# Layer 0's last hidden chunk: a split moved forward, the last sums by output chunk, one written order for three engines

## The chip, the cores and the metric

The kernel runs on one core of a Trainium2 chip, in one launch. The metric is the device time of that launch in microseconds (us): 423.62 us before, the median of three runs (423.48 to 424.63). The engines are called PE (matmul), PEld (its weight loads), DVE (vector), ACT (scalar), POOL and SP. POOL and SP do little here but issue DMAs.

## The reference, cut to what matters

Eight sequences of 128 tokens with 512 features, so 1024 rows, go through two layers:

```python
# layer 0: a linear map with low-rank experts, then a gated FFN with 4-bit weights
c = x @ W.T + low_rank(x)                        # 512 features
g, u = split(c @ dequant(qweight_gu))            # 1376 hidden units each
x = x + (silu(g) * u) @ dequant(qweight_down)
# layer 1: one of 8 matrices for each sequence, RMS norm, then a gated FFN
a = x[b] @ weight[adapter_ids[b]].T
x = x + (silu(n(a) @ gate_w.T) * (n(a) @ up_w.T)) @ down_w.T     # 1792 hidden units
```

## The kernel before

All activations lie feature by row: `xT` is 128 partitions x 4 feature chunks (`KC = 4`) x 1024 rows. The rows are two blocks (`NTB = 2`) of 512 (`TB`). Products are made in rounded halves: a value is split in a high part (ACT) and a low part (DVE), and each product is then two matmuls, one for each part.

The hidden units of layer 0 are 11 chunks of 128 (the last one has 96). For a chunk j, `gu_products` sums gate and up over four feature chunks c, four matmuls for one of gate or up at one c (two parts by two row blocks). The scales of the 4-bit weights differ from one c to the next, so between two c the sum in PSUM is multiplied in place (`rescale`) by a ratio, on ACT or DVE, whichever has the smaller load by the planner's own costs. After the last c, `gu_final` makes the silu on ACT (L675) and the product with up on DVE (L678): this is h(j). `queue_split` puts the two halves of h(j)'s split into the queues of ACT (high part, L323) and DVE (low part, L313). A queued step is written where `pump` finds room for it, or where `flush(name)` demands it at the latest.

The down sums of chunk k are added to four PSUM tiles (one for each output chunk m, with two banks, one for each row block). `down_product` makes four matmuls for one m and one k: both parts by both row blocks. `rescale` stands between two k here too. `down_final` (L719) adds the finished sum to `xT` on DVE.

The function `last_chunk_and_down` interleaves the last chunk's gate and up (j = 10) with the last block of down sums (k = 8, 9, 10). There are four pairs of PSUM banks in all, and gate, up, and the sums of m = 0 and 1 take them; m = 2 gets gate's pair when silu has read it, m = 3 gets up's pair when h(10) is made. Its order is: c = 0; `first(0)` (the products of k = 8 for m = 0 and their rescale); c = 1; `first(1)`; c = 2; `second(0)` (k = 9); c = 3; `second` and `first` for the rest; the split of h(10); a table load on ACT (L776); and at last the products of k = 10, by row block and then by m, each with a final of 512 columns.

Layer 1 begins with eight `adapt` products (L1261, float32), one for each sequence, into single PSUM banks that are the halves of the old pairs. A row's sum goes through a square sum (ACT L1277), a root, a reciprocal (DVE L1286), a scaling (ACT "nx" L1199), four transposes (PE L1302), and a norm. The order of all this, and of the chunk work behind it, comes from a planner (`Plan.run`) that knows a cost and a due time for each task; the first weight splits of layer 1 (L1069 on ACT, L1072 and L1075 on DVE) are ready to run early and fill DVE around the seam of the layers. `sums_of_weights` (L1065, L1066) adds rows of a raw weight buffer on DVE; it needs an accumulating DMA (`add_to_raw`, L1062) that POOL issues. There are three raw buffers, raw0 to raw2. POOL issues the loads of layer 1's matrices too (`load_w1`, L397), into four buffers w1_0 to w1_3; w1_3's place is that of layer 0's h and comes free with the last down product.

What sets the order of the instructions: within a `tc.manual_schedule` the order on PE, DVE and ACT is that of the code, or that in which the planner calls the tasks. SP's and POOL's orders are a scheduler's. There are two such contexts, one for all of layer 0 and one for `plan.run()`.

Of the kernel before, what the change touches and what calls it, by code (L numbers as in the profile page):

```python
# [14 lines left out]
F32 = mybir.dt.float32  # L15
# [8 lines left out]
P = 128  # L24
B, T, D = 8, 128, 512
NT = B * T
TB = 512
# [186 lines left out]
def network_in(ctx, tc, a, out, by_groups, flag, again):  # L214
# [23 lines left out]

    cond_stack, h_stack, w1_stack, ad_stack = (ExitStack() for _ in range(4))
    cp = cond_stack.enter_context(tc.tile_pool(name="cond", bufs=1, side="right"))  # L240

    def behind(inst, other):

# [44 lines left out]
    def spent(n):  # L288

        base = clock[0]  # L290
        clock[0] += 0.2326 * n
        pump(base, clock[0] + OVER)

    def rescale(ps, by):
        n = ps.free_size()
        engine = min(load, key=lambda e: max(load[e], clock[0] + AFTER) + took(e, n))
        charge(engine, took(engine, n))
        if engine == "act":
            nc.scalar.activation(ps, ps, AF.Copy, scale=by)  # L299
        else:  # L300
            nc.vector.tensor_scalar(ps, ps, by, None, ALU.mult)
# [271 lines left out]
    def by_groups_of_scales():  # L573
# [126 lines left out]
                        if half == 1:  # L700
                            queue_split(f"h{j}", h, h2[j])

        def down_product(ps, m, k, first, tbs=range(NTB)):
            n = CH0[k]
            for i in range(2):
                for tb in tbs:
                    nc.tensor.matmul(  # L707
                        ps[:, tb],
                        lhsT=wds[k][:n, m * P : (m + 1) * P],
                        rhs=h2[k][i][:, tb],  # L710
                        start=(first and i == 0),
                        stop=(i == 1),
                        skip_group_check=not first,
                    )
            spent(2 * len(tbs))

        def down_final(x, m, ps, group):
            charge("dve", took("dve", ps.free_size()))
# [16 lines left out]
        def last_chunk_and_down():  # L735
# [35 lines left out]
            for m in range(2, KC):  # L771
# [7 lines left out]
            second(1, range(1, NTB))  # L779
            for m in range(2, KC):  # L780
                second(m)
            for tb in range(NTB):
                for m in range(KC):
                    down_product(sums[m], m, j, False, range(tb, tb + 1))
                    down_final(xT[:, m, tb * TB : (tb + 1) * TB], m, sums[m][:, tb], group)

        def split_condition(tb, ps, i):

# [25 lines left out]
            return count  # L814


        with tc.manual_schedule(engines={EngineType.PE, EngineType.DVE, EngineType.Activation}):

            nc.scalar.activation(root, eps, AF.Exp)
            exp0 = experts(0)  # L820
            x_high(0)
            x_low(0)
            x_scaled(0)
            exp1 = experts(1)
            for m in range(2):
                w_high(m)
            hg0 = gated(0, rows_of(exp0))
            for m in range(2, KC):
                w_high(m)
            kept = cp.tile([P, 2, 2 * (E + E * R)], F32, name="kept")  # L830
            nc.scalar.copy(kept, exp1[:, :, : 2 * (E + E * R)])
            x_high(1)
            scale_bT()
            pairs0, base0 = base_sums()
            for m in range(KC):
                base_products(base0, 0, m, 0)
            hgT0 = turned(hg0, exp0[:, 0, :])
            for m in range(KC):
                w_low(m)
                base_products(base0, 0, m, 1)  # L840
            x_low(1)
            x_scaled(1)
            for ps in pairs0:
                rescale_base(ps)
            pairs1, base1 = base_sums()
            for i in range(2):
                for m in range(KC):
                    base_products(base1, 1, m, i)
            x_diff(0)
            for m in range(KC):  # L850
                w_diff(m)
                base_products(base0, 0, m, 2)
            hg1 = gated(1, [kept[:, i].rearrange("p (b n) -> p b n", b=2) for i in range(2)])
            for ps in pairs1:
                rescale_base(ps)
            x_diff(1)
            queue_zeros(0, 4, "zeros")
            for j in range(4):
                queue_weights(j, f"w{j}")
            flush("w0")  # L860
            for i in range(2):
                for m in range(2 * i, 2 * i + 2):
                    low_rank(base0, hgT0, m)
                split_condition(0, pairs0[i], i)
            ratios(ratio, sc)
            flush("w1")
            ratios(ratio_d, scd)
            for m in range(2):
                base_products(base1, 1, m, 2)
            hgT1 = turned(hg1, base0[0])  # L870
            base_products(base1, 1, 2, 2)
            for i in range(2):
                for m in range(2 * i, 2 * i + 2):
                    if m == KC - 2:
                        base_products(base1, 1, KC - 1, 2)
                    low_rank(base1, hgT1, m)
                split_condition(1, pairs1[i], i)
                if i == 0:
                    for _ in range(2):
                        run("dve", 0)  # L880
            cond_stack.close()
            open_rw()
            pools["w1"] = w1_stack.enter_context(tc.tile_pool(name="w1", bufs=1, side="right"))
            hp = h_stack.enter_context(tc.tile_pool(name="h0", bufs=1, side="right"))
            load_down(*BLOCKS0[0])
            for pair0 in PAIRS0[2:4]:
                load_qw(*pair0)

            def dequantise(pair0, zeros=None):
                if zeros is not None:  # L890
                    queue_zeros(*zeros, "zeros")
                for j in range(*pair0):
                    queue_weights(j, f"w{j}")

            def ready(pair0):
                for j in range(*pair0):
                    flush(f"w{j}")

            load["act"], load["dve"] = clock[0] + 1.0, clock[0] + 2.0

            queue_down(*BLOCKS0[0], "d0", at=clock[0] + 7.0)
            gate_up_pair(0, 1)
            ready(PAIRS0[1])
            dequantise(PAIRS0[2], (4, 8))
            gate_up_pair(2, 3)
            flush("d0")
            load_down(*BLOCKS0[1])
            dequantise(PAIRS0[3])
            queue_down(*BLOCKS0[1], "d4", at=clock[0] + 6.0)
            down(*BLOCKS0[0])  # L910
            ready(PAIRS0[2])
            load_qw(*PAIRS0[4])
            gate_up_pair(4, 5)
            ready(PAIRS0[3])
            load_qw(*PAIRS0[5])
            flush("d4")
            load_down(*BLOCKS0[2])
            dequantise(PAIRS0[4], (8, 10))
            first_raw()
            gate_up_pair(6, 7)  # L920
            dequantise(PAIRS0[5], (10, 11))
            queue_down(*BLOCKS0[2], "d8")
            queue("dve", "indices", 1.7, indices)
            down(*BLOCKS0[1])
            flush("indices")
            first_w1()
            ready(PAIRS0[4])
            gate_up_pair(8, 9)
            ready(PAIRS0[5])
            count = []  # L930
            queue("dve", "verdict", 1.3, lambda: count.append(verdict()))
            queue_first_weights("l1")
            last_chunk_and_down()
            flush("verdict")
            flush("l1")

            def met(ps):
                nc.tensor.matmul(ps[:1, :1], lhsT=count[0][:, 0:1], rhs=count[0][:, 1:2], start=True, stop=True)

            def told(ps):  # L940
                nc.vector.tensor_scalar(flag[:1], ps[:1, :1], float(NGOOD * P), None, ALU.is_lt)

            judges.append((met, told))


    def in_float32():
# [852 lines left out]
```

## Time and profile before

| | |
|---|---|
| median of three runs | 423.62 us (423.48 to 424.63) |
| the profiled execution's own time | 423.74 us |
| its span in the trace | 421.9 us, granted PE clock 0.995 |
| PE busy | 411.8 us (98%) |
| DVE busy | 373.0 us (88%) |
| ACT busy | 307.0 us (73%) |
| layer 0's last chunk and down sums | about 144.8 to 165.6 us of the span |
| layer 1's eight rows (adapt, norm, transposes) | about 165.6 to 205 us |
| layer 1's chunks | about 205 us to the end |

1.84 us of the profiled time lie outside the span. Stretches and single instructions are told in us from the span's start. A line of the timeline gives start, duration, engine, line, operation, output and inputs, shape and count; the bracket at its end is the idle time of that engine ahead of it, and what ended the idle time. A PE line's end is modelled, and short stalls of PE show better on PEld, whose next load can't start while it waits for a semaphore.

### The profile page before, as it was taken

The numbers are of one execution on the slowest core, as the hardware profiler recorded it, in microseconds if no ns is written. First come the engines' busy times: TensorE is split into PE (matmuls) and PEld (weight loads), VectorE is DVE, ScalarE is ACT, GpSimd is POOL, SyncE is SP. The second block draws the span as 40 slices with busy tenths as digits, with TensorE's granted clock in tenths as the row PEclk, the third lists the DMA queues.
The fourth block names the chain that finished last, engine by engine and source line by source line (L and its number), as shares of the span: only waits on it lengthen the run. The fifth ranks groups of instructions, "written<-read, shape, count | busy, mean of one in ns | idle before, by whom it ended". The sixth has DMA issues, their size and how long they took to land.

```text
span 421.9 us, 5201 instructions
## 1 busy us (share of the span) xinstructions
PE 411.8 (98%) x1771; PEld 314.9 (75%) x1771; DVE 373.0 (88%) x678; ACT 307.0 (73%) x503; POOL 27.1 (6%) x34
## 2 busy tenths in 40 slices
PE   8999999999999999999999999999999999999993
PEld 8885778888888765445676777788778877887772
DVE  4799979997998689989999999988998899979963
ACT  5833798868796765668998787658975797669651
POOL 1000200000000300320011011011011001000000
PEclk9999999999999999999999999999999999999997
DMA  8931811010010720870163035033323134000014
GB/s 271 394 144 36 233 56 44 11 53 2 0 62 2 278 46 18 329 239 2 58 181 62 0 87 138 0 87 88 113 50 89 62 75 114 0 3 1 24 51 155
DMA packets 16913, 38.59 MB, mean 91 GB/s; under 512 B 1904, under 2 KB 8432, under 8 KB 15856
## 3 DMA queue, kind: packets, MB, share of 16 engines
q1 hardware_dynamic: 11344, 25.09, 17.8%
q0 software_dynamic: 4960, 12.06, 11.5%
q10 hardware_dynamic: 576, 1.05, 0.6%
q8 instruction: 15, 0.25, 0.2%
q14 instruction: 18, 0.15, 0.1%
HBM read 36.10 MB, written 2.10 MB: 91 GB/s over the span
## 4 chain that ended last, share of the span: by engine, by line
PE 85%; DVE 8%; ACT 4%; issue 1%; ACTq 0%; DVEq 0%
PE bank L1446 27%; PE bank L1585 17%; PE gate L659 9%; PE up L659 9%; PE down L707 8%; PE base L510 5%; PE bank L1261 5%; PE experts L413 2%; PE base L536 2%; DVE w L1072 1%; DVE xT L719 1%; DVE w L1075 1%; PE idle L366 1%; PE bank L1302 1%; DVE snap L1534 1%
## 5 line engine op out<-in xcount | busy, mean ns | idle before, releaser
L1199 ACT ACTIVATE bank<-bank 128x512 f32<-128x512 f32 x129 | 73.3, 584 | 31.9 <-PE bank L1446 17.6
L1585 PE MATMUL bank<-h,d 128*128 128x512 f32 x240 | 66.5, 391 | 0.2
L1585 PEld LDWEIGHTS bank<-h,d 128*128 128x128 f32 x240 | 44.8, 188 | 10.6 <-DVE snap L1480 0.6
L659 PE MATMUL gate<-a,dq 128*128 128x512 f32 (+1 forms) x176 | 47.8, 393 | 0.1
L659 PE MATMUL up<-a,dq 128*128 128x512 f32 (+1 forms) x176 | 47.4, 391 | 0.0
L1446 PE MATMUL bank<-xs,w 128*128 128x512 f32 x168 | 46.0, 396 | 0.8 <-ACT bank L1199 0.8
L1446 PE MATMUL bank<-a,w 128*128 128x512 f32 x168 | 45.2, 394 | 0.2 <-ACT snap L1199 0.2
L707 PE MATMUL down<-h,wd 128*128 128x512 f32 (+1 forms) x176 | 42.6, 395 | 0.6 <-DVE h L313 0.4
L707 PEld LDWEIGHTS down<-h,wd 128*128 128x128 f32 (+1 forms) x176 | 32.4, 188 | 10.0 <-DVE xT L719 1.3
L659 PEld LDWEIGHTS gate<-a,dq 128*128 128x128 f32 (+1 forms) x176 | 32.5, 185 | 8.5 <-ACT sl L675 0.6
L659 PEld LDWEIGHTS up<-a,dq 128*128 128x128 f32 (+1 forms) x176 | 32.4, 185 | 7.9 <-DVE a L791 0.4
L1446 PEld LDWEIGHTS bank<-xs,w 128*128 128x128 f32 x168 | 31.1, 188 | 9.1 <-ACT bank L1199 1.6
L1446 PEld LDWEIGHTS bank<-a,w 128*128 128x128 f32 x168 | 30.7, 188 | 9.0 <-ACT snap L1199 2.2
L1075 DVE SCALAR_TENSOR_TENSOR w<-w 128x512 fp32r<-128x512 f32 x50 | 34.5, 690 | 2.1
L299 ACT ACTIVATE gate<-gate,ratio 128x1024 f32<-128x1024 f32 (+1 forms) x24 | 26.1, 1086 | 10.7 <-PE gate L659 10.7
L1480 DVE SCALAR_TENSOR_TENSOR snap<-bank,snap 128x512 f32<-128x512 f32 x42 | 28.6, 684 | 4.9 <-ACT wz L1069 4.8
L1072 DVE TENSOR_TENSOR w<-raw,w 128x512 fp32r<-128x512 f32 x42 | 28.7, 684 | 3.1 <-ACT w L1069 3.1
L1062 POOL DMA_DIRECT2D raw<-in_wgu x14 | 17.4, 1246 | 208.2 <-PE gate L659 45.6
L1624 DVE SCALAR_TENSOR_TENSOR xT<-bank,xT 128x512 f32<-128x512 f32 (+1 forms) x41 | 27.4, 672 | 3.0 <-PE bank L1585 2.6
L1585 PE MATMUL bank<-w,d 128*128 128x512 f32 x96 | 29.4, 391 | 0.0
L1261 PE MATMUL bank<-w,xT 128*128 128x512 f32 x64 | 29.2, 596 | 0.0
L1199 ACT ACTIVATE snap<-bank 128x512 f32<-128x512 f32 x41 | 24.2, 593 | 5.9 <-PE bank L1446 5.8
(169 smaller groups left out, 736.9 us busy)
## 6 DMA issues: line engine op xcount, KB each, us to landing
raw<-in_wgu SPq DMA_DIRECT2D x14, 640.0 KB, 4.0
raw<-in_wgu POOLq DMA_DIRECT2D x14, 256.0 KB, 4.4
wd<-in_wd SPq DMA_DIRECT2D x14, 256.0 KB, 2.7
qw<-in_qw_gu SPq DMA_DIRECT2D x5, 512.0 KB, 4.7
xT<-in_xT SPq DMA_DIRECT2D x2, 1024.0 KB, 12.2
out<-xT SPq DMA_DIRECT2D x7, 256.0 KB, 2.0
xb<-in_xb ACTq DMA_DIRECT2D x4, 256.0 KB, 5.2
xb<-in_xb SPq DMA_DIRECT2D x4, 256.0 KB, 5.2
```

The costliest lines, as they stand in the source:

```text
L299: nc.scalar.activation(ps, ps, AF.Copy, scale=by)
L510: nc.tensor.matmul(base[m], lhsT=wT3[i][:, m, c * P : (c + 1) * P], rhs=x_parts(tb)[i][:, c, :], start=(i == 0 and c == 0), stop=(i == 1 a ...
L659: nc.tensor.matmul(ps, lhsT=dqs[j][:, c, half, :], rhs=a3[i][:, c, tb * TB : (tb + 1) * TB], start=(c == 0 and i == 0), stop=(i == 1), ski ...
L707: nc.tensor.matmul(ps[:, tb], lhsT=wds[k][:n, m * P : (m + 1) * P], rhs=h2[k][i][:, tb], start=(first and i == 0), stop=(i == 1), skip_gro ...
L1072: nc.vector.tensor_tensor(lo, raw, hi.bitcast(F32), ALU.subtract)
L1075: nc.vector.scalar_tensor_tensor(di, lo.bitcast(F32), -1.0 / EPS, hi.bitcast(F32), ALU.mult, ALU.add)
L1199: nc.scalar.activation(out_, in_, AF.Copy, scale=by)
L1261: nc.tensor.matmul(of("bank", "ad", b), lhsT=xT[:, c, b * T : (b + 1) * T], rhs=of("w1", b)[:, c * D : (c + 1) * D], start=(c == 0), stop= ...
L1446: nc.tensor.matmul(ps, lhsT=w[:, i, n, c * P : (c + 1) * P], rhs=x[i][:, c0 + c], start=(first and i == which[0] and c == 0), stop=True, s ...
L1480: nc.vector.scalar_tensor_tensor(x, of("bank", j, bank_), by, x, ALU.mult, ALU.add)
L1585: nc.tensor.matmul(of("bank", *who), lhsT=of("d", j)[:, i, m * P : (m + 1) * P], rhs=h_tile(j, tb)[:, i], start=(i == 0 and j == j0), stop ...
L1624: nc.vector.scalar_tensor_tensor(x, of("bank", *who)[:, q * w : (q + 1) * w], -EPS, x, ALU.mult, ALU.add)
```

## The change

Three edits. (1) In `last_chunk_and_down`, the products of `first(0)` are parted: those with h(8)'s high part stay behind c = 0, those with its low part go behind c = 1. The split of h(9) is demanded ahead of c = 1, where it was demanded ahead of `second(0)`. And `second(0)` is parted by row blocks: one half stands ahead of the last gate products, the other ahead of the last up products. (2) The last products (k = 10) go by m and not by row block first: four matmuls for an m, then its final over 1024 columns at once; only m = 3 has two finals of 512. (3) One `manual_schedule` is opened at layer 0's start and closed behind `plan.run()`; the code between keeps its order.

```diff
+    order_stack = ExitStack()
+
+    def written_order():
+        engines = {EngineType.PE, EngineType.DVE, EngineType.Activation}
+        order_stack.enter_context(tc.manual_schedule(engines=engines))
...
-        def down_product(ps, m, k, first, tbs=range(NTB)):
+        def down_product(ps, m, k, first, tbs=range(NTB), parts=range(2)):
...
-            def gate_up(c):
-                for half, ps in enumerate(gu):
+            def gate_up(c, halves=range(2)):
+                for half in halves:
+                    ps = gu[half]
...
-            def first(m):
-                down_product(sums[m], m, j - 2, True)
-                rescale(sums[m], ratio_d[:, m, j - 2 : j - 1])
+            def first(m, parts=range(2)):
+                down_product(sums[m], m, j - 2, True, parts=parts)
+                if 1 in parts:
+                    rescale(sums[m], ratio_d[:, m, j - 2 : j - 1])
...
             gate_up(0)
-            first(0)
+            first(0, range(1))
+            flush(f"h{j - 1}")
             gate_up(1)
+            first(0, range(1, 2))
             first(1)
             gate_up(2)
             flush(f"h{j - 1}")
-            second(0)
-            gate_up(3)
+            second(0, range(1))
+            gate_up(KC - 1, range(1))
+            second(0, range(1, NTB))
+            gate_up(KC - 1, range(1, 2))
...
-            for tb in range(NTB):
-                for m in range(KC):
-                    down_product(sums[m], m, j, False, range(tb, tb + 1))
-                    down_final(xT[:, m, tb * TB : (tb + 1) * TB], m, sums[m][:, tb], group)
+            for m in range(KC):
+                down_product(sums[m], m, j, False)
+                if m < KC - 1:
+                    down_final(xT[:, m, :].rearrange("p (b t) -> p b t", b=2), m, sums[m], group)
+                else:
+                    for tb in range(NTB):
+                        down_final(xT[:, m, tb * TB : (tb + 1) * TB], m, sums[m][:, tb], group)
...
-        with tc.manual_schedule(engines={EngineType.PE, EngineType.DVE, EngineType.Activation}):
+        written_order()
...
-    with tc.manual_schedule(engines={EngineType.PE, EngineType.DVE, EngineType.Activation}):
-        plan.run()
+    if not by_groups:
+        written_order()
+    plan.run()
+    order_stack.close()
```

How that moves instructions, by the order of the two programs, engine by engine. PE: the parted products, and the last sixteen by m. DVE: the low part of h(9) stands right behind that of h(8), ahead of the rescale of gate's second sum (c = 1) and of the down rescale of m = 0, which change places too; and the "di" step of a layer 1 weight split (L1075) that stood behind the eight finals stands ahead of the five. ACT: one high part of a layer 1 weight split (L1069) goes two instructions later. POOL: the accumulating DMA into raw2, which was issued ahead of w1_3's first load, is issued behind it. SP is the same, and so is everything in layer 1 on PE, DVE and ACT.

More of the change, by code (lines that the diff above doesn't have):

```diff
@@ L701, in gate_up_pair @@
                             queue_split(f"h{j}", h, h2[j])
-        def down_product(ps, m, k, first, tbs=range(NTB)):
+        def down_product(ps, m, k, first, tbs=range(NTB), parts=range(2)):
             n = CH0[k]
-            for i in range(2):
+            for i in parts:
                 for tb in tbs:
@@ L714, in down_product @@
                     )
-            spent(2 * len(tbs))
+            spent(len(parts) * len(tbs))
         def down_final(x, m, ps, group):
@@ L814, in verdict @@
             return count
-        with tc.manual_schedule(engines={EngineType.PE, EngineType.DVE, EngineType.Activation}):
[L819 to L834, printed above, removed]
-            for m in range(KC):
[L836 to L858, printed above, removed]
-                queue_weights(j, f"w{j}")
[L860 to L943, printed above, removed]
@@ new lines, in by_groups_of_scales @@
+        written_order()
+        nc.scalar.activation(root, eps, AF.Exp)
+        exp0 = experts(0)
+        x_high(0)
+        x_low(0)
+        x_scaled(0)
+        exp1 = experts(1)
+        for m in range(2):
+            w_high(m)
+        hg0 = gated(0, rows_of(exp0))
+        for m in range(2, KC):
+            w_high(m)
+        kept = cp.tile([P, 2, 2 * (E + E * R)], F32, name="kept")
+        nc.scalar.copy(kept, exp1[:, :, : 2 * (E + E * R)])
+        x_high(1)
+        scale_bT()
+        pairs0, base0 = base_sums()
@@ new lines, in by_groups_of_scales @@
+        for m in range(KC):
+            base_products(base0, 0, m, 0)
+        hgT0 = turned(hg0, exp0[:, 0, :])
+        for m in range(KC):
+            w_low(m)
+            base_products(base0, 0, m, 1)
+        x_low(1)
+        x_scaled(1)
+        for ps in pairs0:
+            rescale_base(ps)
+        pairs1, base1 = base_sums()
+        for i in range(2):
+            for m in range(KC):
+                base_products(base1, 1, m, i)
+        x_diff(0)
+        for m in range(KC):
+            w_diff(m)
+            base_products(base0, 0, m, 2)
@@ new lines, in by_groups_of_scales @@
+        hg1 = gated(1, [kept[:, i].rearrange("p (b n) -> p b n", b=2) for i in range(2)])
+        for ps in pairs1:
+            rescale_base(ps)
+        x_diff(1)
+        queue_zeros(0, 4, "zeros")
+        for j in range(4):
+            queue_weights(j, f"w{j}")
+        flush("w0")
+        for i in range(2):
+            for m in range(2 * i, 2 * i + 2):
+                low_rank(base0, hgT0, m)
+            split_condition(0, pairs0[i], i)
+        ratios(ratio, sc)
+        flush("w1")
@@ new lines, in by_groups_of_scales @@
+        ratios(ratio_d, scd)
+        for m in range(2):
+            base_products(base1, 1, m, 2)
+        hgT1 = turned(hg1, base0[0])
+        base_products(base1, 1, 2, 2)
+        for i in range(2):
+            for m in range(2 * i, 2 * i + 2):
+                if m == KC - 2:
+                    base_products(base1, 1, KC - 1, 2)
+                low_rank(base1, hgT1, m)
+            split_condition(1, pairs1[i], i)
+            if i == 0:
+                for _ in range(2):
+                    run("dve", 0)
@@ new lines, in by_groups_of_scales, with dequantise @@
+        cond_stack.close()
+        open_rw()
+        pools["w1"] = w1_stack.enter_context(tc.tile_pool(name="w1", bufs=1, side="right"))
+        hp = h_stack.enter_context(tc.tile_pool(name="h0", bufs=1, side="right"))
+        load_down(*BLOCKS0[0])
+        for pair0 in PAIRS0[2:4]:
+            load_qw(*pair0)
+        def dequantise(pair0, zeros=None):
+            if zeros is not None:
+                queue_zeros(*zeros, "zeros")
+            for j in range(*pair0):
+                queue_weights(j, f"w{j}")
@@ new lines, in ready @@
+        def ready(pair0):
+            for j in range(*pair0):
+                flush(f"w{j}")
+        load["act"], load["dve"] = clock[0] + 1.0, clock[0] + 2.0
+        queue_down(*BLOCKS0[0], "d0", at=clock[0] + 7.0)
+        gate_up_pair(0, 1)
+        ready(PAIRS0[1])
+        dequantise(PAIRS0[2], (4, 8))
+        gate_up_pair(2, 3)
+        flush("d0")
+        load_down(*BLOCKS0[1])
+        dequantise(PAIRS0[3])
+        queue_down(*BLOCKS0[1], "d4", at=clock[0] + 6.0)
+        down(*BLOCKS0[0])
@@ new lines, in by_groups_of_scales @@
+        ready(PAIRS0[2])
+        load_qw(*PAIRS0[4])
+        gate_up_pair(4, 5)
+        ready(PAIRS0[3])
+        load_qw(*PAIRS0[5])
+        flush("d4")
+        load_down(*BLOCKS0[2])
+        dequantise(PAIRS0[4], (8, 10))
+        first_raw()
+        gate_up_pair(6, 7)
+        dequantise(PAIRS0[5], (10, 11))
+        queue_down(*BLOCKS0[2], "d8")
+        queue("dve", "indices", 1.7, indices)
+        down(*BLOCKS0[1])
+        flush("indices")
+        first_w1()
+        ready(PAIRS0[4])
@@ new lines, in by_groups_of_scales, with met, told @@
+        gate_up_pair(8, 9)
+        ready(PAIRS0[5])
+        count = []
+        queue("dve", "verdict", 1.3, lambda: count.append(verdict()))
+        queue_first_weights("l1")
+        last_chunk_and_down()
+        flush("verdict")
+        flush("l1")
+        def met(ps):
+            nc.tensor.matmul(ps[:1, :1], lhsT=count[0][:, 0:1], rhs=count[0][:, 1:2], start=True, stop=True)
+        def told(ps):
+            nc.vector.tensor_scalar(flag[:1], ps[:1, :1], float(NGOOD * P), None, ALU.is_lt)
@@ L946, in in_float32 @@
+        judges.append((met, told))
     def in_float32():
```

## The prediction

> **What bounds the kernel now.** The page first: PE is busy for nearly the whole span, and the chain of waits agrees.
>
> ```profile
> PE 411.8 (98%) x1771; PEld 314.9 (75%) x1771; DVE 373.0 (88%) x678; ACT 307.0 (73%) x503; POOL 27.1 (6%) x34
> PE 85%; DVE 8%; ACT 4%; issue 1%; ACTq 0%; DVEq 0%
> ```
>
> No matmul is removed by the change, so its worth is what it does to PE's waits; those that DVE and ACT end at the seam of the layers, 145 to 172 us, are all it touches. The timeline of PE there, the second view, shows the stall that the first edit removes (147.66), and the gate sum of c = 2 that will matter (150.97).
>
> ```profile
> 146.60 0.62 PE L707 MATMUL down<-h,wd 128*128 128x512 f32 x2
> 147.66 0.73 PE L707 MATMUL down<-h,wd 128*128 128x512 f32 x2 [0.43 <-DVE h L313]
> 148.23 1.08 PE L659 MATMUL gate<-a,dq 128*96 128x512 f32 x4
> 150.97 1.17 PE L659 MATMUL gate<-a,dq 128*96 128x512 f32 x4
> ```
>
> The third view is the timeline of DVE and ACT: the two L313 are the low parts of h(8) and h(9), with a rescale of gate at 149.63 between them; the high part of h(9) is ACT's at 148.00. From 161.53 DVE runs with no pause through the eight finals (L719) and six weight steps to the reciprocal at 171.26, which the first row's "nx" on ACT waits for.
>
> ```profile
> 146.39 1.22 DVE L313 TENSOR_TENSOR h<-h,h 128x1024 fp32r<-128x1024 f32 x1
> 148.00 1.05 ACT L323 ACTIVATE h<-h 128x1024 fp32r<-128x1024 f32 x1
> 149.63 1.28 DVE L301 TENSOR_SCALAR gate<-gate,ratio 96x1024 f32<-96x1024 f32 x1
> 150.82 1.21 DVE L313 TENSOR_TENSOR h<-h,h 128x1024 fp32r<-128x1024 f32 x1
> 152.17 1.29 DVE L301 TENSOR_SCALAR gate<-gate,ratio 96x1024 f32<-96x1024 f32 x1
> 156.16 1.27 DVE L678 SCALAR_TENSOR_TENSOR h<-up,small,sl 96x1024 f32<-96x1024 f32 x1
> 161.53 0.69 DVE L1072 TENSOR_TENSOR w<-raw,w 128x512 fp32r<-128x512 f32 x1 [0.41 <-ACT w L1069]
> 162.14 5.36 DVE L719 SCALAR_TENSOR_TENSOR xT<-down,small,xT 128x512 f32<-128x512 f32 x8
> 171.26 0.16 DVE L1286 RECIPROCAL ss<-ss 128x1 f32<-128x1 f32 x1
> 171.46 0.69 ACT L1199 ACTIVATE nx<-bank,ss 128x512 f32<-128x512 f32 x1 [1.13 <-DVE ss L1286]
> ```
>
> The fourth is PEld at the last sums. Two loads, then 0.36 us of waiting for a final: the second row block's products go at the finals' pace, 0.66 us for 0.45 us of work, and the first adapt waits as well. The last line is the first row's transposes, behind "nx".
>
> ```profile
> 164.25 0.30 PEld L707 LDWEIGHTS down<-h,wd 96*128 96x128 f32 x2 [0.36 <-DVE xT L719]
> 164.91 0.30 PEld L707 LDWEIGHTS down<-h,wd 96*128 96x128 f32 x2 [0.36 <-DVE xT L719]
> 165.57 0.30 PEld L1261 LDWEIGHTS bank<-w,xT 128*128 128x128 f32 x2 [0.36 <-DVE xT L719]
> 172.20 0.42 PEld L1302 LDWEIGHTS bank<-ident,nx 128*128 128x128 f32 x4 [1.18 <-ACT nx L1199]
> ```
>
> **First edit, up to h(10).** Matmuls are 0.227 us apart (four: 0.91). With the low half of `first(0)` gone, gate of c = 1 no longer waits for h(8)'s low part, only for its own rescale, ACT 146.00 to 147.07 in the timeline: it begins at 147.15, not 148.23, and up at 148.15. PE has gained 1.1 us; eight products and six down products bring it to 150.45.
>
> But DVE is asked for h(9)'s low part right behind h(8)'s, which ends at 147.61. Its high part ends on ACT at 148.00 + 1.05 = 149.05 and can't be sooner, since ACT is full from 145.06. So DVE stands still for 1.45 us and starts at 149.08. Queued behind it is the rescale of gate's second sum, ready since 148.35: it starts 1.15 us later, at 150.23, not 149.63, and ends at 151.5. PE's gate of c = 2 starts at 151.55, not 150.97: the gain of 1.1 us has become a wait of 1.1 us and a loss of 0.58. The Trainium skill states that the queues of ScalarE and VectorE are strict first in, first out ("PSUM — Partial Sum Buffer", section "Engine vs sequencer instructions"); this rule speaks against the edit, and if the rescale could overtake, the edit would gain some 0.4 us instead. In the trace no DVE instruction overtakes another, so the loss stands.
>
> It does not shrink. The down rescale of m = 0 stands next on DVE (1.2, until 152.7); gate's c = 2 products end at about 152.75, and their rescale starts at 152.8, not 152.17. PE waits for it until 154.1 (0.25; two of the k = 9 products lie ahead), makes gate of c = 3 until 155.45, two products more, and up until about 156.9, where it was 156.05. The silu starts 0.5 late and ends at 156.55. DVE's small steps between (152.17 to 156.16, nearly all busy) give 152.8 + 4.0 = 156.8. The latest of the three, up, lets h(10) begin at 156.9 instead of 156.16: 0.75 us late, with 0.6 (DVE's own row) and 0.85 (up's) as its ends.
>
> **Behind h(10).** Its high part, the table load, the weight's high part on ACT, and the rescale and low part on DVE are a chain of single steps with no slack; all come 0.75 later, as does the first k = 10 product (161.1 by h(10)'s low part, 159.91 + 1.21): 161.85.
>
> **Second edit.** PE's sixteen products now run unpaced: 16 x 0.227 = 3.63, to 165.5, where the adapt began at 165.57. So PE gains 0.85 here, and its 0.75 is made good. I let the waits on the finals go because a final reads all of its m and no product of that m follows. The skill says that engines on different PSUM banks run clean together and that guards go by bank (same page, "PSUM bank collisions raise a hardware error"); the old wait was between two banks of one pair, so it was the program's, and by this rule too it goes with the order.
>
> DVE is what counts next. From L1072 at 161.53 to the weight step behind the finals (168.01) it took 6.48. Now: L1072 and the dependent L1075 moved up, 0.72 + 0.61 (as at 168.01 to 169.34); three finals of 1024, 1.2 apart (1276 ns each by group, less the overlap of 0.08 that the 512 ones show: 743 ns, 0.66 apart); two of 512, 1.32. Sum 6.25, a gain of 0.23. With the start 0.75 late, DVE is 0.52 late. The finals end at 164.85, 166.05, 167.25, 167.95: adapt's four products (0.86 each from 165.5) wait 0.1 once, for the third, and the first row is summed at 169.1, was 169.0. Its root is ready at about 170.4, but the reciprocal has six weight steps ahead of it on DVE and comes at 171.78. "nx" and the transposes: 172.7, not 172.20. PE has 0.5 us more of waiting there, which is where its gain of 0.85 goes.
>
> From 172 on nothing is changed on PE, DVE and ACT. DVE is busy 31.54 of 35 us from 170 to 205 (the windows), ACT then 5.0 of 5, so I let the 0.5 stand to the end.
>
> **Third edit.** One context instead of two moves nothing on the three engines; on POOL it puts raw2's accumulating DMA (140.53) behind w1_3's load (166.11 + 1.04), which waits for the last down product. Who needs raw2: DVE's third L1065, at 177.15. In the trace that DMA took 10.7 us behind three matrix loads, landing 1.25 us behind the last of them; now one load is ahead (issue to landing 5.6 us, so 171.7): 173 is the estimate, 4 us of slack. Were it 10.7 again, 167.2 + 10.7 = 177.9, against a need at 177.65: 0.25 us. It also sends 256 KB through the stretch 170 to 185, where the DMA engines are 81 to 95% busy, about 1 us for the loads behind; no wait of PE for a matrix stands in the list of waits, so I take nothing. Issuing fits POOL's gap of 2.39 us ahead of 169.54.
>
> **Sum.** +0.75 (h(10) late) - 0.23 (DVE's finals) = +0.52 us. Its ends: -0.25 (0.6 late, and PE keeps its 0.85) and +0.85 (up's delay, nothing won on DVE). On the profiled 423.74 (span 421.9 and 1.84 around it) that is 424.25; the median stands 0.12 below that execution: **424.1 us**, own range 423.4 to 424.5. A measurement of this kernel can tell about 0.3% (1.27 us) from no change, so this counts as the same.
>
> **Rivals.** (a) The gain that the edit is written for, chance 0.18: h(9)'s low part doesn't hold the rescale up, because ACT comes to its high part sooner than the old trace shows. The end of ACT's high part decides: at 148.45 (0.6 earlier) gate of c = 2 loses nothing, before that it gains up to 0.43, the stall removed. Then -0.23 to -0.85: 422.8 to 423.4. Against it: ACT is gapless there. (b) The POOL swap, chance 0.15: raw2 lands after 177.65, DVE stops at its third sum, and each further us costs one, since 5.36 us of finals and the whole row stage show no spare on DVE. Landing at 179: 424.1 + 1.35 = 425.5. For it: the DMA share and the 10.7 us; against it: one load ahead, not three. (c) The clock: PE's new wait before gate of c = 2 might lower it. The wait of 1.18 us at 172.20 has the clock at 1.00 in all windows of 5 us; I give it nothing. The skill ("TensorE: Matmul & The Clock Gate", "What's actually happening") has the clock halved after an idle window of about 3.4 us, an estimate of 1.7 us lost if it came to that; no run here shows it.
>
> **How the numbers follow.** Forecast 0.55, (a) 0.18, (b) 0.15, other causes 0.12. Under 422.35 (faster by over 0.3%) lie 0.05 of (a) and 0.04 of the rest; over 424.89, 0.10 of (b) and 0.08 of the rest. So faster 0.09, same 0.73, slower 0.18. The range takes in (a) but for its far end and (b) up to 1.2 us: 422.9 to 425.3.
>
> **What would show it.** Right: DVE idle for about 1.4 us ahead of the second L313; PE idle for about 1.1 us ahead of a gate sum near 151.5 and none near 147; L678 near 156.9; no PEld wait for L719 among the products of 96 rows; the first reciprocal near 171.8. Wrong: gate of c = 2 before 151; the third L1065 waiting for a DMA; or a shift that changes after 175 us.

## The result, and the profile after

| | before | changed |
|---|---|---|
| median | 424.15 us (22 runs) | 424.79 us (22 runs) |
| ratio | | 1.002 [1.0011, 1.0029], or +0.85 us [0.47, 1.23] |
| profiled execution | 423.74 us, span 421.9 | 424.69 us, span 422.9 |
| granted PE clock | 0.995 | 0.996 |

The change costs 0.64 us by the medians and 0.59 by the traces (below), less than the 0.3% (1.27 us) that the prediction counts as the same: the forecast case (+0.52). The ratio's 0.85 stands above these because of one run of 428.63 us: the means are 0.81 apart with it and 0.63 without. In the page the totals hardly move: PE still carries the chain, 81% of it where it was 85%, with ACT's share up from 4% to 7%.

```profile
PE 412.1 (97%) x1771; PEld 315.9 (75%) x1771; DVE 372.9 (88%) x675; ACT 307.2 (73%) x503; POOL 26.9 (6%) x34
PE 81%; DVE 8%; ACT 7%; issue 1%; DVEq 0%; ACTq 0%
```

The two spans can't be subtracted as they stand. The instructions up to the seam are the same in both programs, yet in the profiled execution after, the product that makes h(8) (L684) begins at 144.23, where before it began at 143.54. These 0.69 us are a difference between the two executions, and 0.67 of it is there before 30 us: the first `base` products with `xd` begin at 28.30 and 27.63. So the readings below are **counted from h(8)'s product**: 0.69 is taken off the times of after before they are set against those of before.

First the timeline of DVE and ACT. The second L319 is h(9)'s low part, behind an idle stretch of 1.47 us that waits for ACT's high part (L329, 148.69 to 149.74). The rescale of gate's second sum is queued behind it (150.91), though its products ended near 149.0. Then come h(10) (L684), the first weight step (L1087), the five finals, and the reciprocal that "nx" waits for.

```profile
147.09 1.22 DVE L319 TENSOR_TENSOR h<-h,h 128x1024 fp32r<-128x1024 f32 x1
148.69 1.05 ACT L329 ACTIVATE h<-h 128x1024 fp32r<-128x1024 f32 x1
149.77 1.23 DVE L319 TENSOR_TENSOR h<-h,h 128x1024 fp32r<-128x1024 f32 x1 [1.47 <-ACT h L329]
150.91 1.28 DVE L307 TENSOR_SCALAR gate<-gate,ratio 96x1024 f32<-96x1024 f32 x1
157.44 1.27 DVE L684 SCALAR_TENSOR_TENSOR h<-up,small,sl 96x1024 f32<-96x1024 f32 x1
162.91 0.69 DVE L1087 TENSOR_TENSOR w<-raw,w 128x512 fp32r<-128x512 f32 x1 [0.50 <-ACT w L1084]
164.25 4.98 DVE L725 SCALAR_TENSOR_TENSOR xT<-down,small,xT 128x1024 f32<-128x1024 f32 x5
172.40 0.15 DVE L1301 RECIPROCAL ss<-ss 128x1 f32<-128x1 f32 x1
172.59 0.69 ACT L1214 ACTIVATE nx<-bank,ss 128x512 f32<-128x512 f32 x1 [1.58 <-DVE ss L1301]
```

The timeline of PE and PEld shows the other side. The wait for h(8)'s low part is gone. A wait for the late rescale stands in its place (152.25), and a smaller one before c = 3 (154.80). The last products run without a wait for a final, but the adapt products now wait for finals three times on PEld, and the first transposes wait 1.63 us, where it was 1.18.

```profile
152.25 1.17 PE L665 MATMUL gate<-a,dq 128*96 128x512 f32 x4 [0.89 <-DVE gate L307]
154.80 0.71 PEld L665 LDWEIGHTS gate<-a,dq 128*96 128x96 f32 x4 [0.44 <-DVE gate L307]
166.06 6.47 PE L1276 MATMUL bank<-w,xT 128*128 128x512 f32 x14
166.77 0.33 PEld L1276 LDWEIGHTS bank<-w,xT 128*128 128x128 f32 x2 [0.53 <-DVE xT L725]
167.97 0.30 PEld L1276 LDWEIGHTS bank<-w,xT 128*128 128x128 f32 x2 [0.86 <-DVE xT L725]
168.62 0.50 PEld L1276 LDWEIGHTS bank<-w,xT 128*128 128x128 f32 x2 [0.36 <-DVE xT L725]
173.33 0.42 PEld L1317 LDWEIGHTS bank<-ident,nx 128*128 128x128 f32 x4 [1.63 <-ACT nx L1214]
```

POOL issues raw2's accumulating DMA behind w1_3's load. It lands 6.4 us after its issue (the DMA list of this stretch), at 173.8. DVE's third sum needs it at 178.29 and shows no wait.

```profile
166.49 0.94 POOL L403 DMA_INDIRECT w<-in_w,row  x1 [25.26 <-PE down L713]
167.43 1.38 POOL L1077 DMA_DIRECT2D raw<-in_wgu  x1
178.29 0.42 DVE L1080 TENSOR_TENSOR raw<-raw 128x256 f32<-128x256 f32 x1
```

### The profile page after: what moved, and what is told of

It reads as the page before. It is cut to its first block, busy times and chain, and to the rows that moved or that the text cites. A ratio compares the mean times of both kernels' runs of the same rounds, so it can differ in the third digit from the quotient of the medians.

```text
span 422.9 us, 5198 instructions
## 1 busy us (share of the span) xinstructions
PE 412.1 (97%) x1771; PEld 315.9 (75%) x1771; DVE 372.9 (88%) x675; ACT 307.2 (73%) x503; POOL 26.9 (6%) x34
## 4 chain that ended last, share of the span: by engine, by line
PE 81%; DVE 8%; ACT 7%; issue 1%; DVEq 0%; ACTq 0%
PE bank L1461 24%; PE bank L1600 17%; PE gate L665 9%; PE up L665 8%; PE down L713 7%; PE base L516 5%; PE bank L1276 5%; PE experts L419 2%; PE base L542 2%; DVE w L1087 1%; DVE w L1090 1%; DVE xT L725 1%; ACT bank L1214 1%; PE idle L372 1%; PE bank L1317 1%
## 5 line engine op out<-in xcount | busy, mean ns | idle before, releaser
L713 PE MATMUL down<-h,wd 128*128 128x512 f32 (+1 forms) x176 | 41.7, 391 | 0.1
L1087 DVE TENSOR_TENSOR w<-raw,w 128x512 fp32r<-128x512 f32 x42 | 28.7, 684 | 3.2 <-ACT w L1084 3.2
```

Source lines behind the costliest of these rows:

```text
L713: nc.tensor.matmul(ps[:, tb], lhsT=wds[k][:n, m * P : (m + 1) * P], rhs=h2[k][i][:, tb], start=(first and i == 0), stop=(i == 1), skip_gro ...
L1087: nc.vector.tensor_tensor(lo, raw, hi.bitcast(F32), ALU.subtract)
```

## The experiments

The theory to be tried (T) is the prediction's: the early low part of h(9) holds up gate's rescale, h(10) comes late, and DVE's order from there to the first reciprocal passes this on, less what the longer finals save. The rivals: the loss comes with the second edit, whose finals the adapt products wait for (W); it is a difference between executions, or of the stretch behind (S); the POOL swap costs (P).

All results in one table, each as a difference from before. The four columns of the traces count from h(8)'s product to h(10)'s, to the first reciprocal, to the last of the eight rows' transposes, and to PE's last product. The last column is the ratio of the runs, turned into us on the median of before (424.15); there are 6 to 12 runs of each experiment.

| kernel | h(10) | reciprocal | eighth row | last product | by the runs, us |
|---|---|---|---|---|---|
| changed | +0.59 | +0.44 | +0.45 | +0.59 | +0.85 [0.47, 1.23] |
| e1, split only | +0.62 | +0.73 | +0.73 | +0.71 | +1.19 [0.72, 1.65] |
| e2, finals only | 0.00 | -0.26 | -0.26 | -0.36 | -0.30 [-0.64, 0.08] |
| e3, two DVE steps back | -0.22 | -0.36 | -0.35 | -0.47 | -0.08 [-0.47, 0.25] |
| e4, late demand | -0.51 | -0.73 | -0.73 | -0.82 | -0.76 [-1.15, -0.38] |
| e5, reciprocal sooner | +0.62 | -0.12 | +0.19 | +0.34 | +1.23 [0.72, 1.74] |
| e6, k = 9 products whole | +0.59 | +0.31 | +0.31 | +0.57 | +0.98 [0.51, 1.40] |
| e7, third edit alone | -0.01 | -0.02 | -0.02 | +0.21 | +0.34 [-0.04, 0.72] |
| e8, both reciprocals sooner | -0.52 | -2.05 | -0.23 | +2.45 | +0.98 [0.47, 1.44] |
| e9, e4 and e5 together | -0.51 | -1.35 | -1.03 | -1.07 | -0.81 [-1.27, -0.38] |
| e10, ACT's high part sooner | +0.42 | +0.28 | +0.29 | +0.85 | +0.55 [0.17, 0.93] |
| e11, finals of 512 | +0.62 | +0.85 | +0.86 | +0.81 | +0.76 [0.38, 1.15] |

**e7: the third edit alone** comes first, since it tells how to read the rest. All engines keep the order of before.

> Before with the third edit alone, the one written order. Every engine's instructions stand in the order of before, POOL's and SP's too. All theories: before + 0.0; what it shows apart from 1.000 is what the comparison of two equal programs can show (0.2 us or less is expected). If the written order did something that the order of instructions doesn't tell, it shows here.

The trace has it equal up to the eighth row (-0.02). Behind that it loses 0.21, where an ACT step in layer 1's first chunk waits for a load, a wait that the trace of before doesn't have:

```profile
214.00 0.63 ACT L1561 ACTIVATE d<-wd 128x512 fp32r<-128x512 f32 x1 [0.18 <-DMA wd<-in_wd]
```

The runs put two programs with equal orders 0.34 us apart, with an interval that reaches zero. So differences of a few tenths in the last column decide nothing by themselves; the counts up to the eighth row do. What comes behind it moves the last product by up to 0.3 in most of these kernels, by 0.56 in e10 (where the same ACT step waits 0.23 for the same load) and by 2.7 in e8. e7 also corrects the prediction on one point: POOL's order here is that of before. The swap of raw2's DMA and w1_3's load is in e2 and not in e1 or e7, so it comes with the second edit, not with the third.

**e1: the split without the new finals; e2: the new finals without the split.**

In e1, against the changed kernel:

```diff
-            for m in range(KC):
-                down_product(sums[m], m, j, False)
-                ...
+            for tb in range(NTB):
+                for m in range(KC):
+                    down_product(sums[m], m, j, False, range(tb, tb + 1))
+                    down_final(xT[:, m, tb * TB : (tb + 1) * TB], m, sums[m][:, tb], group)
```

In e2, against the changed kernel:

```diff
-            first(0, range(1))
-            flush(f"h{j - 1}")
+            first(0)
             gate_up(1)
-            first(0, range(1, 2))
...
-            second(0, range(1))
-            gate_up(KC - 1, range(1))
-            second(0, range(1, NTB))
-            gate_up(KC - 1, range(1, 2))
+            second(0)
+            gate_up(3)
```

> The changed kernel with its second edit undone: the last products go by row block again, with eight finals of 512 columns; the parted products and the early split stay. Theory T (the early low part of h(9) holds up gate's rescale, h(10) is late, DVE's shorter finals give a little back): h(10) as late as in the changed kernel (0.6 us behind before), nothing given back on DVE, so before + 0.6 to 0.8 us (424.8 by the 424.15 of before's median), 0.2 slower than the changed kernel, and the first reciprocal 0.6 to 0.8 behind before's. Rival W (the loss comes with the second edit: the adapt products wait for finals of 1024 columns, 1.7 us of PEld waits against 0.4): this kernel is at or below before, -0.4 to +0.1. Rival S (the 0.6 us are a difference between executions, not the order): within 0.2 of before.

> Before with the second edit alone (last products by output chunk, finals of 1024 columns; the one written order and POOL's swap come with it). Theory T: h(10) as before; DVE's stretch from the finals' start to the next weight step 0.23 shorter; PE's 0.85 at the last products is lost again at the adapt products and at the first transposes, so before - 0.25 us, first reciprocal 0.25 earlier. Rival W (waits of adapt on the long finals cost): +0.2 to +0.6. If PE's gain were kept: -0.85. Rival P (raw2's accumulating DMA behind w1_3 costs): +0.3 or more, with a DMA wait at DVE's third sum.

e1 is late by what T gives, +0.73 by the count; its runs allow 0.72 to 1.65. e2 is early by T's amount, -0.26, and its runs agree. W wanted the opposite of both, and it falls. S, which had e1 within 0.2 of before, falls with e1. In e2 the adapt products wait for the long finals as they do in the changed kernel, and the reciprocal is 0.26 early all the same:

```profile
162.57 4.98 DVE L725 SCALAR_TENSOR_TENSOR xT<-down,small,xT 128x1024 f32<-128x1024 f32 x5
165.09 0.45 PEld L1272 LDWEIGHTS bank<-w,xT 128*128 128x128 f32 x2 [0.41 <-DVE xT L725]
166.28 0.30 PEld L1272 LDWEIGHTS bank<-w,xT 128*128 128x128 f32 x2 [0.74 <-DVE xT L725]
170.91 0.69 ACT L1210 ACTIVATE nx<-bank,ss 128x512 f32<-128x512 f32 x1 [1.59 <-DVE ss L1297]
```

PE begins the adapt products 0.79 earlier than before by the count (the prediction's 0.85), and all but 0.26 of it ends in the wait for "nx". P falls with e2 as well: it has the swap, and no loss.

**e3: two DVE instructions exchanged.** Where the changed kernel demands both parts, ACT's queue is run up to h(9)'s high part, and DVE's up to its low part. That one is taken from the queue and written behind the rescale; its load stays booked, so that no other step changes its engine.

```diff
             first(0, range(1))
-            flush(f"h{j - 1}")
-            gate_up(1)
...
+            low = queues["dve"].pop(0)
+            load["dve"] = max(load["dve"], clock[0] - 0.3) + low[1]
+            gate_up(1, range(1))
+            low[3]()
+            gate_up(1, range(1, 2))
```

> The changed kernel with two DVE instructions exchanged and nothing else: the rescale of gate's second sum (c = 1) stands ahead of h(9)'s low part again. Theory T: PE's wait of 0.89 us before gate of c = 2 goes, the 0.43 us stall of before stays gone too; h(10) begins about 0.3 us earlier than before and 0.9 earlier than in the changed kernel; with the finals' 0.1 to 0.25 the time is before - 0.4 us, 0.9 below the changed kernel. Rival W or S: the same as the changed kernel within 0.2 us, since the rescale would not be what makes it late. PE's order is the changed kernel's.

```profile
149.41 1.29 DVE L307 TENSOR_SCALAR gate<-gate,ratio 96x1024 f32<-96x1024 f32 x1 [0.80 <-PE gate L665]
150.61 1.21 DVE L319 TENSOR_TENSOR h<-h,h 128x1024 fp32r<-128x1024 f32 x1
154.27 0.70 PEld L665 LDWEIGHTS gate<-a,dq 128*96 128x96 f32 x4 [0.72 <-DVE gate L307]
156.94 1.28 DVE L684 SCALAR_TENSOR_TENSOR h<-up,small,sl 96x1024 f32<-96x1024 f32 x1
```

The rescale follows its products at once, and PE has no wait before gate of c = 2 (the wait shown, 0.72 on PEld, stands before c = 3). h(10) is 0.81 earlier than in the changed kernel and the eighth row 0.80 (0.9 expected). By the runs it is before's equal, within an interval that holds the expected -0.4 and lies below that of the changed kernel. So one pair on one engine turns the change from a loss into a small gain by the trace. The Trainium skill has the queues of ScalarE and VectorE as strict first in, first out ("PSUM — Partial Sum Buffer", "Engine vs sequencer instructions"); this pair agrees: in the changed kernel the rescale came at 150.91 behind the low part, though its products had ended near 149.0.

**e4: the demand behind c = 1.**

```diff
             first(0, range(1))
-            flush(f"h{j - 1}")
             gate_up(1)
+            flush(f"h{j - 1}")
```

> The changed kernel with the demand for h(9)'s split moved behind the products of c = 1; by the planner's loads the engines of four rescales change then too (gate's second and third sums are rescaled on ACT, up's second and third on DVE), and the small steps of the verdict go to where DVE stood idle. Theory T: DVE's idle 1.45 us is filled, no rescale stands behind the low part, h(10) begins 0.6 us earlier than before, so before - 0.75 us (1.3 below the changed kernel), the first reciprocal 0.75 earlier. Rival (the stretch behind 172 us is bound by DVE and DMA whatever comes before): the gain at 160 us is gone by 175 us and the time is before's within 0.2 us.

```profile
149.97 1.29 DVE L307 TENSOR_SCALAR up<-up,ratio 96x1024 f32<-96x1024 f32 x1 [0.53 <-PE up L665]
151.18 1.21 DVE L319 TENSOR_TENSOR h<-h,h 128x1024 fp32r<-128x1024 f32 x1
156.21 1.27 DVE L684 SCALAR_TENSOR_TENSOR h<-up,small,sl 96x1024 f32<-96x1024 f32 x1
```

The idle stretch of DVE is filled, h(10) is 0.51 earlier than before, and the eighth row 0.73. The runs say the same, ratio 0.9982 [0.9973, 0.9991]. Both kernels are beaten, though before by less than 0.3%. The rival, that the stretch behind takes all of it back, falls. Two things differ from the changed kernel here, the place of the low part and the engines of four rescales; how much each gives isn't separated. The order alone is what e3 tries.

**e10: ACT's high part one rescale earlier** tries the condition of rival (a).

```diff
-            gate_up(0)
-            first(0, range(1))
-            flush(f"h{j - 1}")
+            gate_up(0, range(1))
+            flush(f"h{j - 1}")
+            gate_up(0, range(1, 2))
+            first(0, range(1))
             gate_up(1)
```

> The changed kernel with two ACT instructions exchanged and nothing else: h(9)'s high part stands ahead of the rescale of up's first sum, 1.0 us earlier. It tries the condition of rival (a) of the prediction, that the end of ACT's high part decides. Theory T: DVE's idle of 1.47 us ahead of h(9)'s low part shrinks to about 0.5, gate of c = 2 waits less, but up of c = 1 now waits for its own rescale some 0.9 longer; h(10) 0.2 earlier than in the changed kernel, the time before + 0.3 us. Rival (a) as the prediction priced it: with the high part ending at 148.1 by before's count (148.45 was the point), the loss is gone: before - 0.2 to - 0.85.

```profile
148.23 1.22 DVE L319 TENSOR_TENSOR h<-h,h 128x1024 fp32r<-128x1024 f32 x1 [0.47 <-ACT h L329]
149.22 0.70 PEld L665 LDWEIGHTS up<-a,dq 128*96 128x96 f32 x4 [1.24 <-ACT up L305]
149.37 1.28 DVE L307 TENSOR_SCALAR gate<-gate,ratio 96x1024 f32<-96x1024 f32 x1
156.72 1.28 DVE L684 SCALAR_TENSOR_TENSOR h<-up,small,sl 96x1024 f32<-96x1024 f32 x1
```

DVE's idle stretch falls to 0.47, and the wait moves: up of c = 1 now waits 1.24 for ACT. h(10) is 0.17 earlier than in the changed kernel, and the time is still above before's. The prediction took the end of ACT's high part as what decides. That end came 1.0 sooner by the count (148.05, where it was 149.05), more than the 0.6 us that it asked for, and most of the loss stayed (+0.42 at h(10)): up's rescale now stands behind the high part, and PE waits for that. So the end of the high part doesn't decide by itself.

**e11: finals of 512 columns**, products by output chunk.

```diff
-                if m < KC - 1:
+                if m < 0:
                     down_final(xT[:, m, :].rearrange("p (b t) -> p b t", b=2), m, sums[m], group)
```

> The changed kernel with the last products by output chunk as they are, but all eight finals of 512 columns again: three more instructions on DVE, PE's order untouched. Theory T: DVE's stretch from the finals to the reciprocal counts, so the reciprocal comes 0.38 later (4.98 becomes 5.36), before + 0.8 to 0.9 us, and from h(8)'s product to the first transposes + 0.8 against before's. Rival W: the adapt products' three waits on finals (0.53, 0.86 and 0.36 on PEld) set the time; finals of 512 for the first row block come earlier, so these waits shrink and the time is the changed kernel's or less, before + 0.2 to 0.6.

```profile
163.66 5.35 DVE L725 SCALAR_TENSOR_TENSOR xT<-down,small,xT 128x512 f32<-128x512 f32 x8
172.38 0.69 ACT L1214 ACTIVATE nx<-bank,ss 128x512 f32<-128x512 f32 x1 [1.79 <-DVE ss L1301]
```

The reciprocal is 0.41 later than in the changed kernel (0.38 expected) and the eighth row too (+0.86). The finals count by DVE's time, not by when a product may start.

**e6: the k = 9 products of m = 0 in one piece.**

```diff
-            second(0, range(1))
-            gate_up(KC - 1, range(1))
-            second(0, range(1, NTB))
-            gate_up(KC - 1, range(1, 2))
+            second(0)
+            gate_up(KC - 1)
```

> The changed kernel with the four k = 9 products of m = 0 in one piece again, ahead of the last gate products; the order on DVE, ACT, POOL and SP is the changed kernel's. Theory T: the 0.44 us wait of PEld before gate of c = 3 is filled by two more products, so up of c = 3 and the time come 0.1 to 0.2 earlier: before + 0.35 us. A rival on which the parting is worth something: slower than the changed kernel by 0.2 to 0.4, since up's last products come two products later.

The wait of 0.44 before gate of c = 3 is gone from the trace. h(10) doesn't move, since DVE's own row sets it (+0.59 both times), and the first reciprocal is 0.13 earlier. The expectation had the gain come with h(10); its size was right, its way was not. The gain arises on ACT: the rescale of a down sum behind the silu is 0.57 late against before, where it is 0.69 late in the changed kernel, and L1085, the first weight step on DVE behind h(10)'s low part (L1087 in the changed kernel), is 0.56 late instead of 0.69. By the runs (+0.98) it can't be told from the changed kernel.

**e5, e8 and e9: the first reciprocal sooner.** Layer 1's planner takes DVE as busy until 2.0 us at its start; a larger number puts fewer weight steps ahead of the reciprocal. The number is 2.5 in e5 (the changed kernel otherwise) and in e9 (e4 otherwise), as in this diff, and 3.5 in e8 (e4 otherwise).

```diff
-    plan = Plan(slots, {"dve": 2.0, "act": 0.3})
+    plan = Plan(slots, {"dve": 2.5, "act": 0.3})
```

> The changed kernel with one number of layer 1's planner changed (DVE taken as busy until 2.5 us, not 2.0, at the planner's start). PE, ACT, POOL and SP keep their order; on DVE the first reciprocal and the small step behind it stand one weight step (about 0.66 us) sooner, and one more weight step of layer 1 comes six places later; nothing else. Theory T, last part (PE's gain of 0.85 at the last products is lost because the first reciprocal stands behind weight steps on DVE): the reciprocal comes 0.6 earlier, the first transposes too, and about half of it is kept behind the eight rows, where DVE has the same work to do: 0.2 to 0.4 below the changed kernel, before + 0.2 us. Rival W (the adapt products, which wait for the long finals, set the time of the first transposes): no change against the changed kernel.

> The late demand for h(9)'s split (the fourth kernel) with the planner's DVE busy until 3.5 us, so that the first two reciprocals stand ahead of several weight steps; layer 1's order behind them changes in places on PE, DVE and ACT, and a little on POOL and SP. Theory T: h(10) 0.6 earlier than before, the first reciprocal some 2 us earlier, of which what DVE has to make up later is lost: before - 1.5 to - 1.8 us if the loads land as they did before, - 0.75 (the fourth kernel's) if the weight steps that were put off are late in turn. Rival: 0 or above, if the weight steps put off hold up the first chunk.

> The fourth kernel (the demand for h(9)'s split behind the products of c = 1) with the fifth kernel's one step on DVE (the first reciprocal ahead of one more weight step). In the traces, counted from the product that makes h(8), the fourth kernel's eighth row of transposes ends 0.73 earlier than before's, and the fifth kernel's 0.26 earlier than the changed kernel's (0.19 against 0.45). Theory T: the two add up, since the reciprocal waits for nothing but its place on DVE: eighth row 1.0 earlier than before's by the same count, time before - 0.9 to - 1.1 us. Rival: the step is lost again in the rows, as most of e8's was: the fourth kernel's time, before - 0.75.

In e5's trace the reciprocal is 0.56 earlier than in the changed kernel and the eighth row 0.26, as expected; that the adapt products set the first transposes is wrong. The runs don't follow: +1.23 where 0.2 was expected. e9's trace has the two moves added up (-1.0 expected, -1.03 found), yet its runs are at e4's level (0.9981 [0.997, 0.9991] against 0.9982), with an interval that holds the expected -0.9 to -1.1 as well as e4's -0.76. So the step on DVE is shown in two traces; e5's runs speak against it, and e9's can't tell. The profiled execution of e5 is the shortest of its six runs (424.59 us, median 425.04), so its trace need not stand for the others; what they lose isn't seen, and this stays open.

e8 was expected 1.5 to 1.8 us below before, or 0.75 if the weight steps put off were late in turn, and came out 0.98 above, where its rival had it. The trace doesn't show the rival's cause, which was weight steps that hold up the first chunk. The gain of 2.05 at the first reciprocal is down to 0.23 by the eighth row. Behind it ACT's table load stands ahead of the rescale that PE waits for; in before that rescale went first (204.95, and the load at 205.58). It is the same kind of exchange again. PE stands for 1.66, and then its clock falls, as the windows show. The first fence is the timeline of ACT and PE, the second the windows, whose last three values are PE's clock, the DMA share and GB/s:

```profile
203.81 1.28 ACT L1391 ACT_TABLE_LOAD   x1
205.73 0.58 ACT L1214 ACTIVATE bank<-bank 128x512 f32<-128x512 f32 x1
206.36 2.76 PE L1461 MATMUL bank<-xs,w 128*128 128x512 f32 x8 [1.66 <-ACT bank L1214]
```

```profile
204.00:206.00 2.00, 0.70 (x4) 0.24 (x2) 1.97 (x6) 1.99 (x4) 0.00 (x0) 1.00 0.00 0
207.00:208.00 1.00, 1.00 (x5) 0.55 (x4) 0.97 (x2) 1.00 (x3) 0.00 (x0) 0.91 0.59 148
208.00:209.00 1.00, 1.00 (x4) 0.81 (x4) 1.00 (x3) 1.00 (x3) 0.00 (x0) 0.50 0.98 389
```

The profiled execution is the longest of e8's ten runs (426.83 us, median 424.93), so the lower clock need not be in all of them.

## Why the prediction was right, step by step

**The wait that takes the place of the stall.** Right to a few hundredths, counted from h(8)'s product: DVE idle 1.47 (1.45 predicted), the rescale at 150.22 (150.23 predicted), gate of c = 2 at 151.56 (151.55), gate of c = 3 at 154.11 (154.1). e3 shows the cause by exchanging the pair alone.

**h(10) late by 0.75** was mis-sized: 0.59 measured, the low end that the prediction gave to DVE's own row. Of the three that it let compete, silu ended at 156.42 and up's products at 156.64, by the same count, and DVE came free last (156.75). That up falls further behind than DVE's row was right (0.81 late, 0.85 predicted), but it doesn't come last. The prediction's end of up before, 156.05, is the silu's end (L675, 154.94 + 1.11), and up's row ends at 155.83; and ten products from 154.1 at its own 0.227 apart end near 156.4, or 156.6 as the view prints a row's end, not 156.9. e6 agrees: with up's products moved, h(10) stays.

**No slack behind it.** Right, but the delay goes on by two ways, and the prediction had one. h(10)'s low part is 0.60 late where h(10) is 0.59 late. ACT's row hangs on PE instead: its rescale of a down sum waits for products that stand behind up's last ones. The first line is before, the second after:

```profile
157.40 1.09 ACT L299 ACTIVATE down<-down,ratio_d 128x1024 f32<-128x1024 f32 x1 [1.35 <-PE down L707]
158.79 1.09 ACT L305 ACTIVATE down<-down,ratio_d 128x1024 f32<-128x1024 f32 x1 [1.67 <-PE down L713]
```

By the count this rescale is 0.69 late, and so are the high part and the table load behind it on ACT, and L1087 on DVE, which waits for ACT. In e6, where up's products come sooner, the rescale is 0.57 late, L1085 0.56 and the reciprocal 0.31, for the same h(10). In e1, where the finals give nothing back, the rescale and the reciprocal are both 0.73 late, for an h(10) that is 0.62 late.

**The second edit: -0.23 on DVE.** Right: the stretch from L1087 to the next weight step is 6.24 (6.25 predicted), e2 gains 0.26 by the count, and e11, which gives the three instructions back, loses 0.41 against the changed kernel. PE's gain was there (adapt begins at 165.37, 165.5 predicted) and ended in the wait for "nx". One term was far off, at no cost: adapt was to wait 0.1 once, and PEld waits 0.53, 0.86 and 0.36. Most of that is a load that stands ready early; PE's own row of 14 products shows no wait and takes 6.47, 0.19 longer than before's 6.28. The first row's square sum on ACT starts at 169.30 by the count, 0.01 earlier than before, where the prediction had the sum 0.1 later. The reciprocal itself: 171.71 (171.78 predicted), transposes 172.64 (172.7).

**The POOL swap.** No cost, as said: landing at 173.1 by the count (173 predicted), needed at 177.6. Its cause was told wrongly: the second edit brings it, as e2 and e7 show.

**The sum.** +0.52 predicted; the trace has +0.45 at the eighth row. Its two terms, where they meet: L1087, from which DVE runs without a pause to the reciprocal, is 0.69 late (0.75 predicted), and the stretch from there is 0.24 shorter (0.23). The first of them is partly luck: 0.75 was h(10)'s delay, taken from times of up that are too late, and h(10) is 0.59 late; the 0.69 comes by ACT's row, which the prediction did not set apart. The further 0.14 at the last product arises near 228 us in layer 1's chunks. The prediction named a shift that changes after 175 us as a sign of being wrong, and by this much it does; e7 shows a drift of that size without any change of order, and what it is in this execution isn't settled.

The absolute figure did less well: 424.1 us predicted, 424.79 measured, above the forecast case's own 423.4 to 424.5 and within the whole range only by the room left for the POOL swap, a rival that fell. Its base was before's median of three runs, 423.62; 22 runs have 424.15, and on that base +0.52 gives 424.67.

**The rivals.** (a) fell: no low part came sooner by itself, and where e10 made ACT's end sooner the wait moved to up. The gain that (a) priced is had by e3 and e4, through DVE's order. (b) fell with DVE's third sum, which doesn't wait. (c) was right to be given nothing here: the clock stays at 1.00 in every window of 5 us from 145 to 175, with PE's waits of 0.89 and 0.80 in them.

## What to carry to other kernels

On an engine that works in order, moving a step ahead moves everything behind it to the end of that step's own wait; find what it is still waiting for and what is queued behind it, before counting the stall that it removes. The same split demanded one stage later (and with it four rescales given to other engines) made 0.76 us less than before out of 0.85 us more, with the same work. And when the expected change is a fraction of a us, count from an event that both programs share: here whole executions were apart by up to 1.3 us before the changed part began.

## What the runs showed of the hardware

The clock. In e8's profiled execution PE stood for 1.66 us after a stretch at full rate, and 1.5 us after it began again its granted clock was 0.50, for about 3.4 us (1.00 up to 207.8, 0.50 to 211.2). Four products took 1.91 us there (1.07 at full clock), so about half of the 3.4 us was lost, as much as the stall itself. In the thirteen traces this is the only fall of the clock that is recorded ahead of PE's last product, and the longest of PE's other waits, 1.01 in e11, left it at 1.00. That the stall caused the fall is inferred from this; no run tried it. The Trainium skill puts such a fall at one idle window or more, of about 3.4 us ("TensorE: Matmul & The Clock Gate", "What's actually happening"). The stall here was about half as long, so by this one execution that figure is no safe bound.

The start. The product that makes h(8) began between 143.25 (e2) and 144.54 (e3) in programs that are alike up to there. The spread is there before 30 us: the first `base` products with `xd` begin at 27.38 in e2 and 28.64 in e3. Which load or wait of the start makes it wasn't followed.
